# Moving small work about in a four-layer graph network: mask rows, one relu, chain distances and small loads

## The chip, the cores and the metric

One core of a Trainium2 chip runs the whole kernel. The metric is the device time of one execution in microseconds, taken as the median of several runs. The engines that matter are TensorE (PE, with its weight loads PEld), VectorE (DVE), ScalarE (ACT), GpSimd (POOL) and SyncE (SP), which issues most DMAs. Each engine works through its own instructions in the order in which the program emitted them.

## What is computed

A node has 64 features, there are 3327 nodes, and a dense 3327 x 3327 adjacency matrix with about half a per cent of non-zero entries is given in full. Four residual layers follow each other, each on a layernorm and relu of the features:

```python
h = relu(layernorm(x)); x = x + relu(ggc(relu(ggc(h, adj, ...)), adj, ...))   # L0: two gated steps
h = relu(layernorm(x)); x = x + ranked(adj) @ (h @ W) + b                      # L1
h = relu(layernorm(x)); x = x + three times: (adj*adj) @ h, then @ W.T + b     # L2
h = relu(layernorm(x)); x = x + twice: tanh(concat([adj @ h, h]) @ W)          # L3
```

`ggc` is a gated unit: m = adj @ (x W), then sigmoid gates r and z, n = tanh(i_n + r h_n), and (1 - z) n + z x. `ranked(adj)` replaces the entries of a row by powers of one half: the last non-zero of the row has the weight 1, the one before it 0.5, and so on for at most 100 of them. So all in all there are eight products with the adjacency matrix or something made from it. The kernel numbers them k = 0 to 7: 0 and 1 are L0, 2 is L1, 3 to 5 are L2, 6 and 7 are L3.

## The kernel before, in words

**Tiles.** The 3327 nodes are padded to 3328, that is 26 blocks of 128. A pair of blocks, b and b + 13, is laid side by side, so the destinations form 13 double blocks, split in four chunks (`CH`) of 3, 3, 3 and 4 double blocks: widths 384, 384, 384 and 512. Chunks 0 and 1 are group 0, chunks 2 and 3 are group 1. A `Tile` is 128 source nodes by all destinations of one group: 128 x 1536 floats (768 KB) for group 0 and 128 x 1792 (896 KB) for group 1. The matrix doesn't fit on the chip, so tiles come from memory again and again: 9 sweeps of 26 tiles, 234 loads, into 20 slots (`dead` is the list of free slots). A slot is free again when its last user has been emitted.

**Stages.** `alone(0, 0)` does product 0 for group 0. Then `joint(g, k)` uses each tile of a group for product k and, some tiles later, for product k + 1, so that one load serves both: group 1 with k = 0 and 1, group 0 with 1 and 2, group 1 with 2 and 3, and so on, till `alone(0, 7)`. The sources of the other group come first, the group's own sources last, since own features of product k + 1 are only known when product k of that group has been finished.

**The ranked product (k = 2).** A mask of a tile (`make_mask`) is 1 where the tile is not 0. It is made by VectorE in two halves (L411), the `pieces`, which wait in a queue and are emitted one by one between the units of work (`mask_pieces`). It has 127 rows of its own; row 128 (L416) gets the number of non-zeros in later blocks, from `totals`, by a DMA that GpSimd issues. TensorE multiplies the mask by a triangular matrix `tri` (L255), which counts non-zeros behind each entry. A relu with a bias then turns the count into the bits of a power of two (`e`), on ScalarE (L461) or on VectorE (L459), and TensorE multiplies it by the features in three bf16 terms (L546). `totals` comes from earlier counting of the masks by TensorE (L481).

**What sets the order.** All engines' orders are written out by `run()` (L652). It walks a list of units (product, chunk, tile): before each it emits loads as far as slots are free, prepares masks up to 44 units ahead, emits `expand` (L255 and the relus) for up to four units ahead, then pieces of masks, then the unit's own matmuls. Beside the units run tasks, written as generators: when one says `yield 2.2`, its next step is emitted as soon as units worth 2.2 us by the code's own costs (`spend`, L322) have been emitted. So a yield is a distance in emission order: it gives the other engines time to finish a step before TensorE comes to the next. A step is emitted at the end of the unit in which its distance runs out. If a result is needed before its task is through, `finish` emits the rest at once.

**The tasks that matter.** `after_0` and `after_1` run when products 0 and 1 of a chunk are complete: `gru` (L781) takes the sum out of PSUM (L741 on ScalarE, L742 on VectorE), makes the gates (L792, L797), r and n (L802, L804, L813) and the new state (L817 to L819). In cell 0 a relu of two halves follows: ScalarE writes one half (L822), VectorE the other (L823), and TensorE transposes both to node order (L707). In cell 1 `after_1` goes on with a transpose (L717, recorded on L255), the residual (L770), the layernorm (`layernorm_relu`, L751 to L765, with the power on GpSimd at L761) and a split of the features in three bf16 terms (`in_three`, L841 on ScalarE and L843 on VectorE). `more_constants` (L190) loads the weights of the cells, `bd` and `w3` (small rows of 256 B, L232 and L234) and the bias rows `brow` (L238), and folds the first weights of a cell into its gates (`fold_cell`). `bd` is first used after product 2, `w3` after product 6 and `brow[:, 0:3]` after product 2.

Of the kernel before, what the change touches and what calls it, by code (L numbers as in the profile page):

```python
# [13 lines left out]
ALU = mybir.AluOpType  # L14
# [81 lines left out]
def kernel(  # L96
# [93 lines left out]
    def more_constants():  # L190
# [38 lines left out]
        load_cell(1)  # L229
        yield 10.0  # L230
        for h in range(2):
            nc.sync.dma_start(out=bd[upper(h), :, upper(h)], in_=weights[:, WL1:WL3])  # L232
            for i in range(2):
                nc.sync.dma_start(out=w3[upper(h), :, i], in_=weights[:, WL3 + (h + i) % 2:NW:2])  # L234
        yield 10.0
        yield from fold_cell(1)
        yield 20.0
        nc.sync.dma_start(  # L238
# [166 lines left out]
    def make_mask(t, kind):  # L405

        t.mask = Mask(t.w)
        rows = P - 1 if kind == RANKED else P

        def piece(half):  # L410
            nc.vector.tensor_scalar(t.mask.view[:rows, half], t.view()[:rows, half], 0.0, None, op0=ALU.not_equal)  # L411
            if half == 0 and kind == RANKED:

                for ch in GROUPS[t.g]:
                    finish(("count", ch))
                nc.gpsimd.dma_start(out=t.mask.view[P - 1:P], in_=totals[t.g][t.q:t.q + D + 1:D, :])  # L416
            if half == 1:
                t.used()

        pieces.extend([(t, 0, piece), (t, 1, piece)])  # L420

# [7 lines left out]
    def expand(k, c, t):  # L429
# [23 lines left out]
        for s in range(2):  # L453
# [3 lines left out]
            busy = any((k - 1, ch) in sums for ch in GROUPS[t.g])  # L457
            if s and (own if t.g == 0 and (own or busy) else c == GROUPS[t.g][1] or t.g == 1 and not own):
                nc.vector.tensor_scalar(wide[:, s], ps[:, :w], BITS, 0.0, op0=ALU.add, op1=ALU.max)  # L459
            else:  # L460
                nc.scalar.activation(wide[:, s], ps[:, :w], AF.Relu, bias=bitsb)  # L461
# [319 lines left out]
    def gru(acc, c, bi, bh, cell, pace=1.0):  # L781
# [37 lines left out]
        nc.vector.tensor_tensor(d, d, r, ALU.add)  # L819
        yield 2.2 * pace  # L820
        if cell == 0:
            nc.scalar.activation(both[c][upper(1), 0], d[upper(1)], AF.Relu)  # L822
            nc.vector.tensor_scalar(both[c][upper(0), 1], d[upper(0)], 0.0, None, op0=ALU.max)  # L823
            yield 1.0 * pace
        return at, d

    parts = {}

    def in_three(h, c):

# [8 lines left out]
        for i in range(2):  # L839
            yield 0.8  # L840
            nc.scalar.copy(terms[i], h)  # L841
# [28 lines left out]
    def after_1(c, acc):  # L870
        pace = 1.0 if c in GROUPS[0] else 1.2
        at, h2T = yield from gru(acc, c, BI2, BH2, 1, pace)
# [134 lines left out]
```

## Time and profile before

| what | value |
|---|---|
| median of three runs | 721.32 us (717.43 to 722.89) |
| the profiled execution | span 714.8 us |
| adjacency tiles loaded | 130 of 768 KB, 104 of 896 KB |
| read from memory | 199.68 MB, 281 GB/s over the span |
| L546 on f32 tiles | 532.6 us busy |
| L546 on the ranked tiles | 72.6 us busy |
| L411, masks on VectorE | 114.8 us busy, 603 ns each |
| L416, rows of masks | 52 DMAs, 31.9 us on GpSimd |

The page gives each engine's busy time and, for each group of instructions, its busy time, the mean length of one and how long the engine had been idle before it, with what ended that wait. Busy times of different engines overlap and don't add up to the span; matmuls overlap each other too. A wait is worth time only where it holds up the engine that sets the end. The timeline of an engine lists its instructions with the start in us from the start of the span, the length, and in brackets the idle time before. Tile and slot names are printed without their numbers: all 20 slots are `adj`, whether they hold a tile, a mask or something of a gated unit.

### The profile page before, as it was taken

The numbers are of one execution on the slowest core, as the hardware profiler recorded it, in microseconds if no ns is written. First come the engines' busy times: TensorE is split into PE (matmuls) and PEld (weight loads), VectorE is DVE, ScalarE is ACT, GpSimd is POOL, SyncE is SP. The second block draws the span as 40 slices with busy tenths as digits, with TensorE's granted clock in tenths as the row PEclk, the third lists the DMA queues.
The fourth block names the chain that finished last, engine by engine and source line by source line (L and its number), as shares of the span: only waits on it lengthen the run. The fifth ranks groups of instructions, "written<-read, shape, count | busy, mean of one in ns | idle before, by whom it ended". The sixth has DMA issues, their size and how long they took to land.

```text
span 714.8 us, 12622 instructions
## 1 busy us (share of the span) xinstructions
PE 685.6 (96%) x5112; PEld 344.0 (48%) x5112; DVE 344.0 (48%) x696; ACT 264.1 (37%) x402; POOL 76.7 (11%) x113
## 2 busy tenths in 40 slices
PE   4999899999999898999999999999999999999997
PEld 1545444555546586545444444334444444334464
DVE  6756636634987988658524102321163566005101
ACT  0114000212037666888998223740065600000101
POOL 3500000001390602121100000000010000000000
PEclk9999999999999999999999999999999999999999
DMA  9999996299586367662999749962998399927991
GB/s 347 401 363 404 405 406 196 64 351 397 186 298 236 115 205 262 211 239 72 313 368 366 255 146 408 405 263 79 375 373 259 113 397 405 404 82 263 403 402 39
DMA packets 69109, 201.54 MB, mean 282 GB/s; under 512 B 7404, under 2 KB 8788, under 8 KB 69052
## 3 DMA queue, kind: packets, MB, share of 16 engines
q1 hardware_dynamic: 66156, 199.70, 75.4%
q8 instruction: 40, 0.66, 0.4%
q10 hardware_dynamic: 720, 0.85, 0.3%
q0 software_dynamic: 2176, 0.20, 0.2%
q14 instruction: 17, 0.14, 0.1%
HBM read 199.68 MB, written 0.85 MB: 281 GB/s over the span
## 4 chain that ended last, share of the span: by engine, by line
PE 55%; DVE 2%; DMA 2%; ACT 0%; issue 0%; POOL 0%; ACTq 0%; DVEq 0%; SPq 0%; POOLq 0%
PE sum L546 51%; PE temp L255 3%; DMA adj<-totals 1%; PE temp L707 1%; DMA adj<-in_adjT 1%; DVE adj L411 1%; DVE both L742 0%; ACT both L741 0%; DVE e L459 0%; POOL st L761 0%; PE sum L255 0%; DVE xs L940 0%; DVE y L765 0%; DVE y L758 0%; DVE t L753 0%
## 5 line engine op out<-in xcount | busy, mean ns | idle before, releaser
L546 PE MATMUL sum<-adj,y 128*64 128x384 f32 (+3 forms) x3016 | 532.6, 503 | 13.2 <-DMA adj<-in_adjT 12.2
L546 PEld LDWEIGHTS sum<-adj,y 128*64 128x64 f32 x3016 | 221.5, 137 | 267.8 <-issue 223.9
L388 ACT ACTIVATE adj<-adj 128x768 f32<-128x768 f32 (+1 forms) x173 | 141.9, 891 | 50.3 <-PE sum L546 26.9
L411 DVE TENSOR_SCALAR adj<-adj 128x768 bf16<-128x768 f32 (+3 forms) x208 | 114.8, 603 | 33.5 <-PE temp L481 29.6
L461 ACT ACTIVATE e<-temp,bitsb 128x384 int16<-128x384 f32 (+1 forms) x114 | 65.3, 606 | 23.5 <-PE temp L255 14.6
L546 PE MATMUL sum<-e,adj 128*64 128x384 bf16 (+1 forms) x624 | 72.6, 339 | 0.6 <-DVE e L459 0.6
L742 DVE COPY both<-sum 64x384 f32<-64x384 f32 (+3 forms) x17 | 9.7, 569 | 118.7 <-ACT both L741 117.5
L741 ACT COPY both<-sum 64x384 f32<-64x384 f32 (+3 forms) x17 | 8.1, 477 | 155.2 <-PE sum L546 155.1
L390 DVE TENSOR_TENSOR adj<-adj 128x768 f32<-128x768 f32 (+1 forms) x35 | 33.6, 1006 | 51.1 <-DMA adj<-in_adjT 30.9
L255 PE MATMUL temp<-adj,tri 128*64 128x384 bf16 (+1 forms) x334 | 51.9, 342 | 5.5 <-DVE e L459 2.3
L761 POOL TENSOR_TENSOR st<-st,mhalf 128x6 f32<-128x6 f32 (+1 forms) x16 | 24.0, 1500 | 295.5 <-DVE st L760 295.5
L546 PEld LDWEIGHTS <-adj 128*64 128x64 bf16 x624 | 40.4, 110 | 18.5 <-issue 6.4
L416 POOL DMA_DIRECT2D adj<-totals x52 | 31.9, 615 | 133.5 <-DVE adj L819 75.0
L459 DVE TENSOR_SCALAR e<-temp 128x384 int16<-128x384 f32 (+1 forms) x53 | 31.8, 606 | 21.2 <-ACT e L461 8.6
L255 PEld LDWEIGHTS <-tri 128*64 128x64 bf16 x416 | 28.6, 109 | 25.8 <-issue 12.8
L736 DVE STREAM_TRANSPOSE both<-y 32x96 f32<-32x96 f32 (+1 forms) x128 | 35.6, 278 | 2.9
L688 DVE COPY t<-sum 128x384 f32<-128x384 f32 x8 | 4.4, 555 | 61.3 <-PE sum L546 61.3
L481 PE MATMUL temp<-adj,behind 128*64 128x384 bf16 x208 | 28.8, 339 | 0.6 <-DVE adj L411 0.4
L686 ACT COPY t<-sum 128x384 f32<-128x384 f32 (+1 forms) x8 | 4.2, 528 | 53.7 <-PE sum L546 53.7
L481 PEld LDWEIGHTS <-behind 128*64 128x64 bf16 x208 | 13.6, 110 | 21.1 <-issue 19.5
L903 DVE TENSOR_TENSOR y<-temp,brow 128x384 f32<-128x384 f32 (+1 forms) x8 | 4.7, 591 | 29.6 <-PE temp L255 29.6
L515 ACT ACTIVATE lastw<-adj,bitsb 128x768 int16<-128x768 f32 (+1 forms) x2 | 2.0, 984 | 44.1 <-DVE adj L513 44.1
(113 smaller groups left out, 330.1 us busy)
## 6 DMA issues: line engine op xcount, KB each, us to landing
adj<-in_adjT SPq DMA_DIRECT2D x130, 768.0 KB, 7.8
adj<-in_adjT SPq DMA_DIRECT2D x104, 896.0 KB, 12.4
xs<-in_x SPq DMA_DIRECT2D x1, 640.0 KB
adj<-totals POOLq DMA_DIRECT2D x26, 3.0 KB, 4.9
adj<-totals POOLq DMA_DIRECT2D x26, 3.5 KB, 3.0
out<-xs ACTq DMA_DIRECT2D x2, 192.0 KB, 4.0
folds<-in_weights SPq DMA_DIRECT2D x4, 64.0 KB, 12.1
out<-xs ACTq DMA_DIRECT2D x1, 256.0 KB
```

The costliest lines, as they stand in the source:

```text
L255: nc.tensor.matmul(out[hs], lhsT[:, hs], rhs, start=start, stop=stop)
L388: nc.scalar.activation(sq, v, AF.Square)
L390: nc.vector.tensor_tensor(sq, v, v, ALU.mult)
L411: nc.vector.tensor_scalar(t.mask.view[:rows, half], t.view()[:rows, half], 0.0, None, op0=ALU.not_equal)
L416: nc.gpsimd.dma_start(out=t.mask.view[P - 1:P], in_=totals[t.g][t.q:t.q + D + 1:D, :])
L459: nc.vector.tensor_scalar(wide[:, s], ps[:, :w], BITS, 0.0, op0=ALU.add, op1=ALU.max)
L461: nc.scalar.activation(wide[:, s], ps[:, :w], AF.Relu, bias=bitsb)
L481: nc.tensor.matmul(counts[c][1][s * D:(s + 1) * D, :w], behind[:, NQ - 1 - t.q:NQ - 1 - t.q + D], t.mask.view[:, s, t.cols(c)], start=firs ...
L546: nc.tensor.matmul(acc[h][1][h * D:(h + 1) * D, :w], yq[h], rhs[h], start=first and n == 0, stop=last and n == len(terms) - 1)
L736: nc.vector.transpose(to[at:at + 32, :, q], h[q * 32:(q + 1) * 32, :, s, f * 32:(f + 1) * 32])
L742: nc.vector.tensor_copy(both[c][upper(1), 1], acc[1][1][upper(1), :width(c)])
L761: nc.gpsimd.tensor_tensor(st[:, 3, :n], st[:, 2, :n], mhalf[:, :n], ALU.pow)
```

## The change

Five edits are made together; none changes what is computed or how many instructions there are.

1. Rows of masks ahead: the DMA that fills row 128 of a ranked mask is issued when the mask is planned (`make_mask`), not when its first piece is emitted.
2. The relu of cell 0: VectorE's half is emitted right behind L819, with no distance between. ScalarE's half stays behind the distance, which becomes 2.4 for 2.2; the one after it no longer scales with `pace`.
3. Relus of the ranked product: in group 1, for own tiles of chunk 2, the second relu of a unit of chunk 2 goes to VectorE. For own tiles of chunk 3 it stays on ScalarE.
4. Longer distances: `after_1` runs with pace 1.25 for all chunks (before: 1.0 in group 0, 1.2 in group 1), and the distance ahead of each copy in `in_three` is 1.2 for 0.8. The aim is that VectorE's work of the two chains of group 0 doesn't crowd the relus of the ranked product.
5. Small rows later: the loads of `bd` and `w3` are moved behind the fold of cell 1 and 40 further; `brow` follows 5 later.

```diff
         yield 50.0
         load_cell(1)
-        yield 10.0
+        yield 20.0
+        yield from fold_cell(1)
+        yield 40.0
         for h in range(2):
             nc.sync.dma_start(out=bd[upper(h), :, upper(h)], in_=weights[:, WL1:WL3])
             for i in range(2):
                 nc.sync.dma_start(out=w3[upper(h), :, i], in_=weights[:, WL3 + (h + i) % 2:NW:2])
-        yield 10.0
-        yield from fold_cell(1)
-        yield 20.0
+        yield 5.0
         nc.sync.dma_start(
             out=brow[:, 0:3],
...
         def piece(half):
             nc.vector.tensor_scalar(t.mask.view[:rows, half], t.view()[:rows, half], 0.0, None, op0=ALU.not_equal)
-            if half == 0 and kind == RANKED:
-
-                for ch in GROUPS[t.g]:
-                    finish(("count", ch))
-                nc.gpsimd.dma_start(out=t.mask.view[P - 1:P], in_=totals[t.g][t.q:t.q + D + 1:D, :])
             if half == 1:
                 t.used()
 
+        if kind == RANKED:
+
+            for ch in GROUPS[t.g]:
+                finish(("count", ch))
+            nc.gpsimd.dma_start(out=t.mask.view[P - 1:P], in_=totals[t.g][t.q:t.q + D + 1:D, :])
         pieces.extend([(t, 0, piece), (t, 1, piece)])
...
-            if s and (own if t.g == 0 and (own or busy) else c == GROUPS[t.g][1] or t.g == 1 and not own):
+            alone = own and chunk_of(t.q % NB) == GROUPS[1][1]
+            if s and (own if t.g == 0 and (own or busy) else c == GROUPS[t.g][1] or t.g == 1 and not alone):
                 nc.vector.tensor_scalar(wide[:, s], ps[:, :w], BITS, 0.0, op0=ALU.add, op1=ALU.max)
...
         nc.vector.tensor_tensor(d, d, r, ALU.add)
-        yield 2.2 * pace
+        if cell == 0:
+            nc.vector.tensor_scalar(both[c][upper(0), 1], d[upper(0)], 0.0, None, op0=ALU.max)
+        yield 2.4 * pace
         if cell == 0:
             nc.scalar.activation(both[c][upper(1), 0], d[upper(1)], AF.Relu)
-            nc.vector.tensor_scalar(both[c][upper(0), 1], d[upper(0)], 0.0, None, op0=ALU.max)
-            yield 1.0 * pace
+            yield 1.0
         return at, d
...
-    def in_three(h, c):
+    def in_three(h, c, pace=1.0):
...
         for i in range(2):
-            yield 0.8
+            yield 1.2 * pace
             nc.scalar.copy(terms[i], h)
...
     def after_1(c, acc):
-        pace = 1.0 if c in GROUPS[0] else 1.2
+        pace = 1.25
         at, h2T = yield from gru(acc, c, BI2, BH2, 1, pace)
```

## The prediction

> **What bounds the kernel now.** I read the page's first part, then the list of TensorE's waits, then the timelines of the engines around each wait, and last the chain of waits.
>
> ```profile
> span 714.8 us, 12622 instructions
> PE 685.6 (96%) x5112; PEld 344.0 (48%) x5112; DVE 344.0 (48%) x696; ACT 264.1 (37%) x402; POOL 76.7 (11%) x113
> ...
> PE sum L546 <- DMA adj<-in_adjT: 12.2, 7, 8.3
> PE temp L255 <- DVE e L459: 2.3, 3, 1.6
> PE temp L255 <- DMA adj<-totals: 2.2, 2, 1.1
> PE sum L707 <- DVE both L823: 2.1, 1, 2.1
> ```
>
> TensorE is busy 96% of the span. It stands for 714.8 - 685.6 = 29.2 us in all, of which 8.3 us are the first load and about 4 us the tail after the last matmul; no edit touches either. What is left, some 17 us or 2.3%, is all that a change of order can win, since no matmul is removed. So each edit is priced by the wait of TensorE that it can end. Four places matter: the relu (77 us), the late tile (130 us), the crowded VectorE (225 to 250 us), and the two waits for rows of masks (285 and 317 us).
>
> The relu, as TensorE and VectorE saw it (start, length, instruction; in brackets the idle time before it and who ended it):
>
> ```profile
> 77.05 0.80 PE L707 MATMUL sum<-ident,both 128*64 128x64 f32 x20 [2.13 <-DVE both L823]
> ...
> 72.23 0.56 DVE L819 TENSOR_TENSOR adj<-adj 128x384 f32<-128x384 f32 x1
> 76.65 0.34 DVE L823 TENSOR_SCALAR both<-adj 64x384 f32<-64x384 f32 x1
> ```
>
> Its input was ready at 72.79, yet it ran at 76.65: VectorE first worked off the next chunk's L817 to L819 and three masks that the code had put before it.
>
> The late tile, with SyncE's issues before it, and the same wait one stage later:
>
> ```profile
> 129.82 0.87 PE L546 MATMUL sum<-adj,y 128*64 128x384 f32 x4 [1.28 <-DMA adj<-in_adjT]
> ...
> 124.08 0.62 SPq L232 DMA_DIRECT2D bd<-in_weights  x1
> 124.75 1.26 SPq L234 DMA_DIRECT2D w<-in_weights  x2
> ...
> 212.40 1.51 PE L546 MATMUL sum<-adj,y 128*64 128x384 f32 x8 [0.75 <-DMA adj<-in_adjT]
> ```
>
> The last adjacency tile of group 1 is issued at about 123.45 us (its issue ends at 124.02), right ahead of six loads of small rows, and lands about 6.3 us later.
>
> The stretch with both of group 0's chains: three of TensorE's waits, then busy time by window.
>
> ```profile
> 234.51 0.35 PE L255 MATMUL temp<-adj,tri 128*64 128x384 bf16 x2 [0.44 <-DVE e L459]
> 235.50 0.35 PE L255 MATMUL temp<-adj,tri 128*64 128x384 bf16 x2 [0.65 <-DVE xs L770]
> 241.36 0.35 PE L255 MATMUL temp<-adj,tri 128*64 128x384 bf16 x2 [1.64 <-DVE e L459]
> 225.00:250.00 25.00, 21.23 (x265) 15.68 (x263) 24.04 (x52) 18.12 (x37) 11.13 (x16) 1.00 0.41 147
> ```
>
> The columns of the last line are the stretch, its length, then PE, PEld, DVE, ACT and POOL. VectorE works 24.04 of 25 us and TensorE only 21.23, so here VectorE is the bound. TensorE's waits between 223 and 250 us sum to 0.22 + 0.44 + 0.65 + 0.58 + 1.64 + 0.20 = 3.7 us.
>
> **What the Trainium skill says.** "PSUM — Partial Sum Buffer", section "Engine vs sequencer instructions": the queues of ScalarE, VectorE and GpSimdE are strictly first in, first out. The relu above agrees: ready at 72.79, run at 76.65. "DMA: Bandwidth & Descriptors", section "Specifications": transfers under 512 B don't reach line rate. The rows of `bd` and `w3` are 256 B each; the tile that shared the queues with them took about 6.3 us where the first load after the quiet stretch, of the same 896 KB, took 5.1 (237.89 to 242.96). The same page, section "Anatomy of one DMA — SWDGE (gpsimd) path", gives a DMA issued from GpSimd about 2.0 us of fixed cost; here the 52 rows of masks took 1.6 us at least, 4.0 in the median, 6.0 at most. So a row must be issued some 4 us ahead to be free.
>
> **The change, part by part.**
>
> *Half of the relu at once.* L823 moves in front of the yield, behind L819. It then ends at 72.79 + 0.34 = 73.13 us. TensorE reaches L707 at 74.5 (its first four matmuls, on ScalarE's half, start at 74.51), so the wait of 2.13 goes. The next chunk's chain slides by 0.34 us, and its own relu half is done at about 76.4, while TensorE, 2.1 us earlier, wants it at 78.70 - 2.13 = 76.6: at most 0.1 us. The yield of 2.4 for 2.2 doesn't move the step, as both run out within the same unit of the schedule. Does the gain last? Adjacency tiles land every 2.2 us, and TensorE spends 3.2 + 0.2 us on one when both layers use it (L546 x16 in 3.18, then L481), so tiles pile up and no load limits it till the late tile, whose issue waits on masks and counts that move with TensorE. **Gain 2.0 us**, between 1.0 and 2.1.
>
> *Small rows later.* The six loads leave the late tile alone. At 5.0 us from issue it lands at 128.5, when TensorE has ended the work before it (129.82 - 1.28 = 128.54): gain 1.28, at least 0.6. Where do they go? Walking the schedule with the code's own costs, load and fold of cell 1 stay where they were, and the six loads come 40 later: between the 75th and the 76th tile load, that of `brow` between the 77th and the 78th. The 78th is the one that lands at 212.40 and is waited for already. SyncE issues the 75th at 198.46 and the 76th at 201.61, so six issues of 0.65 us each (124.08 to 128.0) push the 76th to about 203.0, and the 78th from 205.62 to 206.2. Their packets took 1.3 us of all 16 DMA engines' time, `brow`'s 0.3, in a stretch whose DMA share was 0.9 to 1.0. So the 78th lands 0.3 to 2.5 us later; I take 1.1, since some of its wait is for slots. **Net gain 0.2 us**, between -1.9 and +1.0.
>
> *Longer distances.* No work is added, only order. In steps of the code, group 0's chain of after_1 takes 6.6 x 1 + 1.2 x 4 + 3.2 + 1.5 = 16.1 before, and 6.8 x 1.25 + 1.5 x 4 + 4.0 + 1.5 = 20.0 after. That is 3.9 more between the end of layer 1's sum and the node features that layer 2 needs. Group 1's grows by 1.6 and has over 10 to spare. What it can win is the 3.7 us above, what limits it is VectorE's total: 24.04 us of work in 25. The longer chain moves about 1.6 us of it (three L843 of 0.54) behind the first unit that needs it, and moves some 2 us of early chain work into the full stretch. What it can lose is the far end: chunk 0's last L843 ends at 244.47, and the first unit that reads it starts at 250.23. Of these 5.8 us the change takes 3.9 and a faster TensorE up to 3.7 more, so a stall of up to 2 us may replace the waits. **Gain 1.2 us**, between -2.0 and +3.5.
>
> *Rows of masks ahead.* Only the place of 52 issues in GpSimd's queue changes; in group 0 by one unit of 0.65, in group 1's last tiles by up to 3.5. Behind an issue that waits for its buffer can stand the power of the layernorm (L761, 1.35 us) and the rows of `lasty`. The two waits for rows come from here:
>
> ```profile
> 281.48 1.32 POOL L761 TENSOR_TENSOR st<-st,mhalf 128x6 f32<-128x6 f32 x1 [7.03 <-DVE st L760]
> 282.76 1.20 POOL L416 DMA_DIRECT2D adj<-totals  x2
> ...
> 312.39 2.39 POOL L416 DMA_DIRECT2D adj<-totals  x4 [8.42 <-ACT e L461]
> ```
>
> The first stood behind L761, which the code emits before that mask is made in either version. The second waited for its buffer, and its mask is made and its first piece emitted in the same turn of run(). Neither is issued earlier. The masks' own VectorE work (L411) never waited for a row, as VectorE's list of waits has none for `totals`, so the turned order adds no wait there. **Gain 0.1 us**, between -0.8 and +2.2.
>
> *Relu of chunk 2's own tiles.* For six units of chunk 2 the second relu goes from ScalarE to VectorE, 0.6 us on either (L461 606 ns, L459 606 ns). TensorE didn't wait for ScalarE there. VectorE has gaps of 1.6 to 3.4 us up to 318 us, few after, and ten masks of 329 us lie on the chain of waits: **loss 0.1 us**, between -0.8 and +0.3 as a gain.
>
> Sum: 2.0 + 0.2 + 1.2 + 0.1 - 0.1 = 3.4 us, or 0.5%. From the median of 721.32 this gives **717.9 us**.
>
> **The rivals.** *Everything ends*: 2.1 for the relu, 1.28 for the tile with nothing paid at 212 us, 3.5 of the chains' waits and 2.2 of the rows'. That is 9.1 us, so 712.2. For it speaks that each named wait has an edit aimed at it; against it, the two rows whose cause isn't touched, and VectorE's 24.04 of 25 us. *New waits take the place of the old*: the relu and the tile win 3.3, but the 78th tile lands 2.5 us later, the first own units stall 3.0 us for features that come late, and the relus on VectorE cost 0.8. That is 3.0 lost, net of the gains: 721.32 - 3.3 + 6.3 = 724.3, slower. For it speaks that both hits fall on waits and margins seen above; against it, that both need the worst bound at once. *Only the relu counts* (2 us, the rest even): 719.3, inside the forecast.
>
> **From the cases to the numbers.** The forecast, with the relu alone as its weak form, gets 0.66, everything ends 0.19, new waits 0.15. The predicted time is the forecast's. The range reaches from 712.5 (nearly the full gain) to 723.0 (past no change): the bounds of the single terms give this, and the three runs before lie 5.5 us apart. Faster by over 1% means under 714.1: most of the second case, 0.14. Slower by over 1% means over 728.5, beyond even the worst sum: 0.04. Within 1%: 0.82.
>
> **What would show it.** Right: no wait of L707 for L823 near 77 us; L546 not waiting near 127 us; a wait for a tile near 209 us of 1 to 3 us; both waits for rows still about 1.1 us each; waits of L255 for L459 and L770 between 220 and 247 us down from 3.7 to about 2.5. Wrong: a wait of the first own unit of layer 2 over 2 us, the rows' waits gone, or a wait of L411 for a row. The forecast fails if tiles turn out to limit TensorE between 80 and 200 us, since then the first 3 us are given back.

## The result, and the profile after

The changed kernel took **724.71 us** (median; 721.83 to 727.44), the kernel before 720.82 us beside it on the same chip. The ratio is **1.0049, 95% interval 1.0034 to 1.0064**: the change made the kernel slower by some 3.5 us. The forecast was 717.9 us, with a range up to 723.0.

Single executions of one kernel lie 6 to 8 us apart here, and the two profiled ones lie at opposite ends: 716.73 us for the kernel before, 727.13 for the changed one. So the traces show which waits there are; what an edit is worth is read from the ratios, which rest on all the executions. The page of the changed kernel, first part:

```profile
span 725.3 us, 12627 instructions
PE 690.7 (95%) x5112; PEld 360.6 (50%) x5112; DVE 346.7 (48%) x702; ACT 261.7 (36%) x396; POOL 76.7 (11%) x113
```

TensorE stands for 725.3 - 690.7 = 34.6 us, where it was 29.2, and it is busy 5.1 us longer with the same 5112 instructions. Part of this second sum is a lower clock, which comes below. The top of the list of TensorE's waits (engine, line, what was waited for: us in all, times, longest):

```profile
PE sum L547 <- DMA adj<-in_adjT: 14.3, 8, 8.3
PE temp L255 <- DMA adj<-totals: 4.9, 2, 3.1
PE temp L255 <- DVE e L460: 2.4, 4, 0.8
```

Lines have moved by one to three: L546 is L547, L459 is L460, L481 is L482, L802 and L804 are L803 and L805, L817 to L819 are L818 to L820, L770 is L771, L823 is L822. The wait of L707 for the relu is gone; waits for tiles and rows have grown, those for `L805` and `L771` have grown or are new. These waits on TensorE's timeline:

```profile
78.23 0.32 PE L482 MATMUL temp<-adj,behind 128*64 128x384 bf16 x1 [0.51 <-DVE adj L411]
128.93 0.87 PE L547 MATMUL sum<-adj,y 128*64 128x384 f32 x4 [0.17 <-DMA adj<-in_adjT]
214.72 2.00 PE L547 MATMUL sum<-adj,y 128*64 128x384 f32 x8 [3.58 <-DMA adj<-in_adjT]
232.54 0.77 PE L255 MATMUL temp<-adj,tri 128*64 128x384 bf16 x4 [2.07 <-DVE adj L805]
245.16 0.35 PE L255 MATMUL temp<-adj,tri 128*64 128x384 bf16 x2 [1.53 <-DVE xs L771]
293.25 0.52 PE L255 MATMUL temp<-adj,tri 128*64 128x384 bf16 x4 [3.05 <-DMA adj<-totals]
326.90 0.52 PE L255 MATMUL temp<-adj,tri 128*64 128x384 bf16 x4 [1.81 <-DMA adj<-totals]
```

**Relu and late tile** did as forecast in the main: 2.13 us became 0.72, now for masks (0.51 here and 0.21 just behind; the forecast had at most 0.1), and 1.28 became 0.17. **The 78th tile** is waited for 3.58 us (and 0.15 just before) instead of 0.75. SyncE's own timeline shows what stands ahead of it:

```profile
197.58 0.54 SPq L353 DMA_DIRECT2D adj<-in_adjT  x1
198.17 0.62 SPq L234 DMA_DIRECT2D bd<-in_weights  x1
198.84 1.26 SPq L236 DMA_DIRECT2D w<-in_weights  x2
200.15 0.61 SPq L234 DMA_DIRECT2D bd<-in_weights  x1
200.80 1.28 SPq L236 DMA_DIRECT2D w<-in_weights  x2
202.19 2.42 SPq L353 DMA_DIRECT2D adj<-in_adjT  x2
204.66 0.60 SPq L238 DMA_DIRECT2D brow<-in_bias_rows  x1
205.35 1.20 SPq L353 DMA_DIRECT2D adj<-in_adjT  x2
```

The 75th is the load issued at 197.58, the 78th the one at 205.35; before, they were issued at 198.46 and 205.62. So the loads run a little earlier here, and counted from the 75th the 78th comes after 7.77 us for 7.16: the 0.6 us that the forecast had for the delay of the issue. The larger part is on its way: in the stretch 195 to 210 us the transfers moved 252, 276 and 316 GB/s before, 235, 239 and 280 after. The middle one of the three stretches, before and after (the last two numbers are the share of the DMA engines and GB/s):

```profile
200.00:205.00 5.00, 5.00 (x38) 2.34 (x34) 5.00 (x11) 2.55 (x6) 4.94 (x8) 1.00 0.84 276
200.00:205.00 5.00, 5.00 (x40) 2.42 (x38) 5.00 (x11) 2.64 (x5) 3.97 (x6) 1.00 0.85 239
```

By 5 us each that is 0.45 MB less, over half a tile, and 0.26 MB of what was moved after are the small rows themselves. So the tiles queued ahead of the 78th, and it with them, come later.

**The chains.** TensorE now waits 2.07 us for `L805`, a reader of a PSUM bank that it wants to write. VectorE's timeline ahead of that wait:

```profile
228.48 0.56 DVE L460 TENSOR_SCALAR e<-temp 128x384 int16<-128x384 f32 x1 [2.72 <-PE temp L255]
229.07 1.12 DVE L818 TENSOR_TENSOR adj<-both,adj 64x384 f32<-64x384 f32 x2
230.22 0.56 DVE L819 TENSOR_TENSOR adj<-adj 128x384 f32<-128x384 f32 x1
230.81 0.56 DVE L820 TENSOR_TENSOR adj<-adj 128x384 f32<-128x384 f32 x1
231.29 0.61 DVE L803 SCALAR_TENSOR_TENSOR adj<-temp,bcol,adj 128x384 f32<-128x384 f32 x1
```

L818 to L820 are the last step of chunk 0's gated unit. Before, VectorE did them at 222.19 to 224.5, ahead of the relu for which it then waited 0.71 us:

```profile
222.19 1.12 DVE L817 TENSOR_TENSOR adj<-both,adj 64x384 f32<-64x384 f32 x2
...
225.21 0.56 DVE L459 TENSOR_SCALAR e<-temp 128x384 int16<-128x384 f32 x1 [0.71 <-PE temp L255]
```

With the longer distances they stand behind that relu: VectorE idles 2.72 us, then works 2.2 us on chunk 0 while chunk 1's L803 and L805, and the bank with them, are held up. Its full stretch doesn't go, it only comes later. In the changed kernel VectorE works 24.54 us of the 25 from 241 us on; in the version without edit 5 (below), where no half clock falls into the stretch, the busy times (VectorE's is the third) are:

```profile
231.00:256.00 25.00, 19.81 (x258) 15.55 (x255) 24.44 (x51) 16.39 (x33) 9.93 (x13) 1.00 0.30 98
```

### The profile page after: what moved, and what is told of

Same layout as the page of the kernel before. It is cut to its first block, busy times and chain, and to the rows that moved or that the text cites. A ratio compares the mean times of both kernels' runs of the same rounds, so it can differ in the third digit from the quotient of the medians.

```text
span 725.3 us, 12627 instructions
## 1 busy us (share of the span) xinstructions
PE 690.7 (95%) x5112; PEld 360.6 (50%) x5112; DVE 346.7 (48%) x702; ACT 261.7 (36%) x396; POOL 76.7 (11%) x113
## 4 chain that ended last, share of the span: by engine, by line
PE 51%; ACT 4%; DMA 2%; DVE 1%; issue 1%; ACTq 0%; DVEq 0%
PE sum L547 47%; ACT adj L388 4%; PE temp L255 3%; DMA adj<-totals 1%; DVE adj L411 1%; PE temp L708 1%; DMA out<-xs 1%; DVE both L743 0%; ACT both L742 0%; DVE xs L942 0%; ACT t L687 0%; PE sum L255 0%; ACT t L939 0%; ACT e L462 0%; ACTq L944 0%
## 5 line engine op out<-in xcount | busy, mean ns | idle before, releaser
L547 PE MATMUL sum<-adj,y 128*64 128x384 f32 (+3 forms) x3016 | 537.1, 505 | 15.2 <-DMA adj<-in_adjT 14.3
L547 PEld LDWEIGHTS sum<-adj,y 128*64 128x64 f32 x3016 | 232.8, 138 | 261.9 <-issue 213.9
L547 PE MATMUL sum<-e,adj 128*64 128x384 bf16 (+1 forms) x624 | 73.6, 342 | 0.6 <-DVE e L460 0.6
L462 ACT ACTIVATE e<-temp,bitsb 128x384 int16<-128x384 f32 (+1 forms) x106 | 61.2, 601 | 34.0 <-PE temp L255 17.8
L547 PEld LDWEIGHTS <-adj 128*64 128x64 bf16 x624 | 41.6, 111 | 18.9 <-issue 6.8
L460 DVE TENSOR_SCALAR e<-temp 128x384 int16<-128x384 f32 (+1 forms) x61 | 36.3, 602 | 23.4 <-PE temp L255 14.2
L482 PE MATMUL temp<-adj,behind 128*64 128x384 bf16 x208 | 31.2, 340 | 1.3 <-DVE adj L411 1.2
L482 PEld LDWEIGHTS <-behind 128*64 128x64 bf16 x208 | 17.7, 111 | 18.4 <-issue 16.7
```

Of the source, the lines that this page charges most:

```text
L482: nc.tensor.matmul(counts[c][1][s * D:(s + 1) * D, :w], behind[:, NQ - 1 - t.q:NQ - 1 - t.q + D], t.mask.view[:, s, t.cols(c)], start=firs ...
L547: nc.tensor.matmul(acc[h][1][h * D:(h + 1) * D, :w], yq[h], rhs[h], start=first and n == 0, stop=last and n == len(terms) - 1)
```

## Single edits

Each edit alone, in the kernel before. Edit 5, small rows later:

```diff
-        yield 10.0
+        yield 20.0
+        yield from fold_cell(1)
+        yield 40.0
         for h in range(2):
             nc.sync.dma_start(out=bd[upper(h), :, upper(h)], in_=weights[:, WL1:WL3])
...
-        yield 10.0
-        yield from fold_cell(1)
-        yield 20.0
+        yield 5.0
```

> The kernel before with the small rows later alone. Theory 'small rows' (the loads of bd, w3 and brow now share the queues with the 78th tile): L546's wait for the late tile near 130 us goes (1.28 to at most 0.3), the wait for the 78th tile near 212 us grows from 0.75 to 3 us or more, and a pause of that length is followed by a stretch of half clock on TensorE of about 3.4 us (some 1.7 us lost): 2 to 4 us slower than before, ratio 1.003 to 1.005. Rivals 'chains' and 'rows': this edit is about even, ratio 0.999 to 1.001.

Edit 2, the relu:

```diff
-        yield 2.2 * pace
         if cell == 0:
-            nc.scalar.activation(both[c][upper(1), 0], d[upper(1)], AF.Relu)
             nc.vector.tensor_scalar(both[c][upper(0), 1], d[upper(0)], 0.0, None, op0=ALU.max)
-            yield 1.0 * pace
+        yield (2.4 if cell == 0 else 2.2) * pace
+        if cell == 0:
+            nc.scalar.activation(both[c][upper(1), 0], d[upper(1)], AF.Relu)
+            yield 1.0
```

> The kernel before with the relu's half at once alone (the distances behind it as in the changed kernel, cell 0 only). All theories: the wait of L707 near 77 us goes; the masks that follow are 0.3 to 0.7 us late for L481, so the gain is 1.2 to 2.0 us: ratio 0.997 to 0.9985.

Edit 4, longer distances:

```diff
-        yield 2.2 * pace
+        yield (2.2 if cell == 0 else 2.4) * pace
...
-            yield 0.8
+            yield 1.2
             nc.scalar.copy(terms[i], h)
...
-        pace = 1.0 if c in GROUPS[0] else 1.2
+        pace = 1.25
```

> The kernel before with the longer distances alone (pace 1.25, 2.4 in cell 1, 1.2 in in_three). Theory 'chains' (a chain that is drawn out holds its PSUM banks for more units, so L255 waits for the bank till L804 or L770 has read it, and then the clock halves): TensorE's waits between the end of product 1 in group 0 and the first own unit rise from 3.7 to about 6 us, with one stretch of half clock: 2 to 4 us slower, ratio 1.003 to 1.006. Theory 'small rows': even, 0.999 to 1.001.

Edit 1, rows of masks ahead:

```diff
-            if half == 0 and kind == RANKED:
-                for ch in GROUPS[t.g]:
-                    finish(("count", ch))
-                nc.gpsimd.dma_start(out=t.mask.view[P - 1:P], in_=totals[t.g][t.q:t.q + D + 1:D, :])
...
+        if kind == RANKED:
+            for ch in GROUPS[t.g]:
+                finish(("count", ch))
+            nc.gpsimd.dma_start(out=t.mask.view[P - 1:P], in_=totals[t.g][t.q:t.q + D + 1:D, :])
         pieces.extend([(t, 0, piece), (t, 1, piece)])
```

> The kernel before with the rows of masks issued ahead alone. Theory 'rows' (the issue order on GpSimd makes rows land later): the two waits for rows, 2.2 us before, become about 4.9 us as in the changed kernel, with half clock behind the longer one: 2.7 to 4.4 us slower, ratio 1.004 to 1.006. Theory 'small rows' or 'chains': waits for rows stay near 1.1 us each, ratio 0.999 to 1.001, and the long waits for rows in the changed kernel come from where tile loads fall in time.

Edit 3, the relus of chunk 2:

```diff
-            if s and (own if t.g == 0 and (own or busy) else c == GROUPS[t.g][1] or t.g == 1 and not own):
+            alone = own and chunk_of(t.q % NB) == GROUPS[1][1]
+            if s and (own if t.g == 0 and (own or busy) else c == GROUPS[t.g][1] or t.g == 1 and not alone):
```

> The kernel before with the fifth part alone: in group 1, the second relu of chunk 2's own tiles on VectorE. Theory 'clock' (the changed kernel is slower mainly because more of TensorE's pauses are long enough to be followed by 3.4 us of half clock; the small rows, the chains and the rows of masks cause them): this part makes no pause, ratio 0.999 to 1.001. Rival 'VectorE is full at 320 us': masks come late, L255 waits for L411 or L459 for 1 to 3 us between 317 and 335 us, ratio 1.002 to 1.004.

| edit alone | ratio to before (95%) | in us | waits in its trace |
|---|---|---|---|
| small rows | 1.0024 (1.0001 to 1.0047) | +1.7 | late tile 0.71; 78th tile 0.99 and 2.39 |
| relu | 0.9962 (0.9941 to 0.9983) | -2.7 | L481 for masks 0.73, in place of L707's 2.13 |
| distances | 1.0014 (0.9993 to 1.0035) | +1.0 | 219 to 262 us: 6.0 for 3.7 |
| rows ahead | 1.0017 (0.9999 to 1.0036) | +1.2 | 219 to 262 us: 4.4; rows 2.93 and 1.77 |
| chunk 2's relus | 0.9997 (0.9978 to 1.0016) | -0.2 | its time alone is used |

The relu alone makes the kernel faster, small rows alone slower, though its interval only just lies above 1; each of the other three can't be told from no change by itself. The five sum to 1.0 us, give or take some 3, so they neither contradict the 3.5 us nor account for them.

## One edit undone, or placed otherwise, in the changed kernel

Four versions of the changed kernel: without edit 5, without edit 4, without edit 1, and with edit 5 only half done, the rows of `bd` and `w3` right behind the fold:

```diff
         yield 20.0
         yield from fold_cell(1)
-        yield 40.0
         for h in range(2):
             nc.sync.dma_start(out=bd[upper(h), :, upper(h)], in_=weights[:, WL1:WL3])
...
-        yield 5.0
+        yield 20.0
         nc.sync.dma_start(
             out=brow[:, 0:3],
```

The other three put the lines of edits 5, 4 and 1 back as they were.

> The changed kernel with the loads of bd, w3 and brow put back to their old places. Theory 'small rows': the wait for the 78th tile falls from 3.7 to about 1.3 us and with it one stretch of half clock; the late tile waits 1 us again: 1 to 3 us faster than the changed kernel, so ratio to the kernel before 1.001 to 1.003. Rival (the sum of the other parts is what costs): ratio 1.004 or more.

> The changed kernel without the longer distances: the pace of after_1 and the distances of in_three are as before. If the chains cost 1.5 to 2 us (waits 5.9 for 3.7 us, and a half-clock stretch of 1.7 us behind the one of 2.07 us), the wait for L805 near 232 us goes and the ratio to the kernel before is 1.001 to 1.003. If they are worth nothing by themselves and the small rows cost everything, it stays at 1.004 to 1.006. If the longer distances gain what was forecast (1.2 us), it rises to 1.006 to 1.007.

> The changed kernel with one edit undone: the row of a mask is issued with the mask's first piece, as before. If the rows ahead cost what they seemed to alone (1.0017, within its interval nothing), the ratio is 1.002 to 1.005; the waits for rows near 293 and 327 us stay, at 1 to 3.5 us each. If the rows ahead are what makes these two waits long, both fall to 1.1 us and the ratio to 1.000 to 1.002.

> The changed kernel with one thing different: the six loads of bd and w3 go right behind the fold of cell 1 (not 40 later), and brow keeps its old distance of 20. If the small rows, by way of the 78th tile, cost what the changed kernel loses, the wait near 215 us falls from 3.58 to about 1.2 us, no half-clock stretch follows it, and the time is 3 to 4 us under the changed kernel: 720.5 to 721.5, a ratio to the kernel before of 0.998 to 1.001. If the chains (waits of L255 for L805 and L771, 5.9 us) cost it, the wait near 215 us may go but the ratio stays at 1.003 to 1.005.

And, from the kernel before, the relu together with the small rows right behind the fold (the two edits already shown):

> The kernel before with the relu's half at once, and with the loads of bd and w3 behind the fold of cell 1 with no further distance: between the 54th and the 55th tile load, brow where it was. Theory 'small rows' (what costs is that they share the queues with a tile that is just in time; tiles 53 to 60 land over 8 us ahead of their use): the late tile's wait near 128 us is at most 0.4 us and the 78th's stays near 1 us; 2 us for the relu and 1 us for the tile, ratio 0.994 to 0.996. Rival (the wait for the 78th tile doesn't come from the small rows): it is again over 2.5 us, ratio 0.998 or more.

| version | ratio to before (95%) |
|---|---|
| changed kernel | 1.0049 (1.0034 to 1.0064) |
| without small rows later | 1.0010 (0.9990 to 1.0031) |
| without longer distances | 1.0019 (1.0000 to 1.0038) |
| without rows ahead | 1.0028 (1.0006 to 1.0049) |
| small rows right behind the fold | 0.9996 (0.9976 to 1.0016) |
| before, with relu and small rows right behind the fold | 0.9967 (0.9945 to 0.9990) |

In company, small rows cost 0.0049 - 0.0010, or 2.8 us, the distances 2.2 and the rows 1.5, each give or take 2, so that the rows may cost nothing. (A second measurement of the changed kernel, below, gave 1.0068; against it each is 1.4 us more.) Moved 40 earlier, the small rows give back the whole loss: late tile 0.42, 78th tile 1.34 us. That confirms the place of the loads as a cause. In this trace, though, the wait at the first row's place is also shorter, 1.20 us for 3.05; since it was 1.17 in a second trace of the changed kernel, this may be chance, and what share of the return it has isn't shown. The loads aren't the only cause: without the distances the wait of 2.07 us went, and the ratio fell as expected for that. Without rows ahead the two waits for rows stayed, at 3.41 and 2.00 us, so this edit isn't what makes them long. And beside the relu, small rows right behind the fold add nothing that can be told: 0.9967 for 0.9962 with the relu alone, whose trace has only 0.31 us left for the late tile.

Which loads delay the 78th tile, `bd` and `w3` or `brow`? In the next one, from the kernel before, the first are loaded after `brow`, which keeps its distance from the fold, so no small row stands right ahead of the 78th tile:

```diff
-        for h in range(2):
-            nc.sync.dma_start(out=bd[upper(h), :, upper(h)], in_=weights[:, WL1:WL3])
-            for i in range(2):
-                nc.sync.dma_start(out=w3[upper(h), :, i], in_=weights[:, WL3 + (h + i) % 2:NW:2])
...
         yield from fold_cell(1)
         yield 20.0
         nc.sync.dma_start(
             out=brow[:, 0:3],
...
+        yield 20.0
+        for h in range(2):
+            nc.sync.dma_start(out=bd[upper(h), :, upper(h)], in_=weights[:, WL1:WL3])
+            for i in range(2):
+                nc.sync.dma_start(out=w3[upper(h), :, i], in_=weights[:, WL3 + (h + i) % 2:NW:2])
```

> The kernel before with one thing different: bd and w3 are loaded after brow, 20 later, and brow keeps its old distance from the fold. If the six loads of bd and w3 (3.9 us of issue ahead of the 76th tile) make the 78th tile late, its wait is about 2.4 to 3 us as with the whole edit, and the ratio is 1.001 to 1.004. If brow, whose 128 small packets lie right ahead of the 78th tile in the changed kernel, makes it late, the wait is 0.75 to 1.5 us as before, the late tile's wait of 1.28 us falls, and the ratio is 0.998 to 1.000.

The ratio was 1.0011 (0.9992 to 1.0030), and on TensorE's timeline:

```profile
214.20 0.89 PE L546 MATMUL sum<-adj,y 128*64 128x384 f32 x4 [2.24 <-DMA adj<-in_adjT]
216.16 2.83 PE L546 MATMUL sum<-adj,y 128*64 128x384 f32 x8 [1.07 <-DMA adj<-in_adjT]
```

3.3 us in all, as with the whole edit (3.4 alone), so the six loads of `bd` and `w3` do it, ahead of the 76th tile; `brow` isn't needed for it. Nor is a late issue: here the 78th is issued 7.17 us behind the 75th, as before. The ratio alone would not have shown it, as its interval includes 1. Over the traces of all kernels run, the waits for tiles at this place come to 3.0 us or more, 3.3 in the mean, in the six with late small rows and no other work put in (changed kernel twice, edit 5 alone, this one, no distances, no rows), and to 0.75 to 2.06 us, 1.4 in the mean, in the ten that load them earlier. So the edit adds 1.9 us there; the 0.75 that the forecast started from was the lowest of all.

## What a long pause does to the clock

Behind three of the pauses above the trace shows a lower clock. Busy time in stretches of the changed kernel (stretch, length, then PE, PEld, DVE, ACT, POOL, granted clock of TensorE, share of the DMA engines, GB/s):

```profile
215.00:220.00 5.00, 5.00 (x24) 2.08 (x22) 2.06 (x4) 1.91 (x4) 0.21 (x1) 0.66 0.78 269
295.00:300.00 5.00, 5.00 (x33) 2.18 (x32) 2.32 (x4) 2.75 (x5) 0.54 (x1) 0.75 0.08 17
```

The records have it as half clock for 3.41 us at a time, from 215.60, 232.67 and 294.11: within 0.9 us behind the waits of 3.58, 2.07 and 3.05 us. Before, there was none but in the tail. To see the cost by itself, VectorE was made to repeat an idempotent maximum in two hops of the kernel before (12 instructions more in all), so that TensorE has to wait where it is otherwise the bound:

```diff
             m = evacuate(acc, c)
+            for _ in range({3: 4, 4: 8}[k] if c == 0 else 0):
+                nc.vector.tensor_tensor(m, m, m, ALU.max)
             yield 0.8
```

> The kernel before with two pauses of TensorE put in where nothing else waits: four extra maxima of VectorE (0.56 us each, they change nothing) on the sum of chunk 0 after product 3, eight after product 4. TensorE waits for them at about 414 us for 1.2 to 1.8 us and at about 438 us for 3.3 to 4.0 us. Theory 'clock': the granted clock stays full after the short pause and is half for 3.4 us after the long one, in which the matmuls of L546 take about twice as long, so the span grows by the pauses and by 1.7 us more. Rival (the half clock comes from something else, such as the amount of work): full clock after both.

TensorE's timeline, then a stretch behind the second pause:

```profile
421.04 0.88 PE L255 MATMUL temp<-bd,t 128*64 128x128 f32 x12 [1.74 <-DVE t L899]
448.61 1.55 PE L255 MATMUL temp<-bd,t 128*64 128x128 f32 x12 [4.11 <-DVE t L899]
```

```profile
448.00:452.00 4.00, 3.39 (x22) 2.22 (x24) 1.11 (x2) 0.00 (x0) 0.00 (x0) 0.58 1.03 406
```

Behind 1.74 us the clock stayed full, behind 4.11 it was halved. The transpose L707 that began at 637.50 us before began at 650.54 here, 13.04 later; ahead of the pauses the lag was 5.42 (L546 at 348.00 and 353.42). Of the 7.62 us between, 5.85 are the pauses themselves and **1.77 the half clock**, near to half of 3.41. It was not caught up. The execution took 729.76 us.

When does it come? The half-clock stretches of one trace all begin on a grid of 3.41 us, which lies otherwise in each execution. In 19 traces (changed kernel twice, all other kernels that were profiled here but one), over 3,767 periods of this grid between 20 and 700 us, I summed TensorE's idle time in each. All 30 periods with 1.98 us or more were followed by one at half clock. Of those with 1.91 us or less only two were, and both were themselves at half clock. So in these traces the limit lies between 1.91 and 1.98 us of idle time within one period, and where the grid lies decides whether a wait of 2 to 3 us falls into one period or is split. L707's wait of 2.13 us was split in the profile of before (1.91 in one period), with no effect, and brought half clock in the kernels with only the rows ahead, and with `brow` kept.

The Trainium skill, "TensorE: Matmul & The Clock Gate", section "What's actually happening", describes this: a clock gate with two states, half and full, set by a free-running activity window of 3413 ns. The traces agree on both numbers. It names an idle window of about 3.4 us as what throttles; here 1.98 us of idle time in it were enough.

## Is the half clock what the change lost?

By the mean granted clock of the timed executions, the changed kernel loses (1 - 0.9924) x 720 = 5.5 us to it, the kernel before 2.3. The difference is nearly the whole loss, so I took it for the cause and tried to remove it with no wait removed: useless matmuls (`ident` by `ident`, into a bank that is overwritten next) right ahead of the matmuls that wait.

```diff
+    def fill(n):
+        i = idle_temps[0]
+        for _ in range(n):
+            mm(banks[i][:, :P], ident, ident)
...
+        if len(rows_of) > 32 and t is rows_of[32] and c == GROUPS[t.g][0]:
+            fill(5)
...
+        if len(loads) > 77 and t is loads[77] and k != COUNT and (k, c) == (1, GROUPS[t.g][0]):
+            fill(7)
```

> The changed kernel with work added and none taken away: right ahead of the matmuls that wait for the 78th tile TensorE does 14 useless matmuls (64x128 f32, ident by ident, into a bank that the next user overwrites), right ahead of those that wait for the first late row 10 of them: by the length of L547 about 1.7 and 1.2 us. They leave the ends of both waits where they were and cut the idle time in them from 3.58 to about 1.9 us and from 3.05 to about 1.9 us. If the half-clock stretches behind these pauses cost time, one or both go, and the kernel with more work is 2 to 3.5 us faster than the changed one: a ratio to the kernel before of 1.000 to 1.002. If the waits alone cost the time and the clock only comes along, it stays at 1.004 to 1.006; if the added work counts, 1.006 to 1.009.

On TensorE's timeline the first filling took 1.70 us, the wait behind it was 2.10, and the half clock at this place was gone:

```profile
210.55 1.70 PE L255 MATMUL temp<-ident 128*64 128x128 f32 x28
214.35 1.51 PE L559 MATMUL sum<-adj,y 128*64 128x384 f32 x8 [2.10 <-DMA adj<-in_adjT]
```

Yet the ratio was 1.0055 (1.0032 to 1.0078), though the mean clock gave back 3.2 us. The next versions were the changed kernel again, three fillings (`fill(6)`, and `fill(4)` ahead of each of the two late rows), and the same three in places where TensorE doesn't wait (`loads[59]`, `rows_of[35]`, `rows_of[38]`):

> The changed kernel, for the same chip and hour as the next two: a ratio to the kernel before of 1.004 to 1.006, half-clock stretches of 3.41 us behind pauses of over 2 us, and waits of 2.5 to 3.7 us for the 78th tile, 2 for L805, 1 to 3.5 for each of the two rows.

> The changed kernel with 12, 8 and 8 useless matmuls right ahead of those that wait for the 78th tile, the first and the second late row: 1.46, 1.0 and 1.0 us of work, by the 1.70 us that 14 of them took. If half clock costs time and the waits are longer than the added work, nearly all of it goes (mean clock 0.998 for 0.992) and the time is 3 to 4 us under that of the changed kernel. If the added work costs what the clock gains, or the time saved is waited for at the next load, the time is within 1 us of it. If the added work is simply added, it is 3 us over it.

> The changed kernel with the same 12, 8 and 8 useless matmuls in other places: ahead of a tile of the third sweep and of the 36th and the 39th mask, where TensorE didn't wait in any profile. The half-clock stretches stay. If TensorE is the bound there, the added 3.5 us are added: a ratio of 1.009 to 1.011 to the kernel before. If the next wait gives them back (a tile or a row that comes at its own time), less: 1.005 to 1.007.

| kernel | ratio to before (95%) | median us | lost to half clock by the mean clock, us |
|---|---|---|---|
| changed kernel again | 1.0068 (1.0043 to 1.0093) | 724.61 | 6.6 |
| three fillings in the pauses | 1.0052 (1.0029 to 1.0076) | 724.09 | 2.0 |
| the same elsewhere | 1.0072 (1.0048 to 1.0095) | 725.85 | 3.4 |

The theory fell in this form: 4.6 us of half clock taken away brought 0.5 us in the median, 1.2 give or take 2.5 by the ratios. And the same fillings elsewhere, which were expected to leave the half clock as it was, went along with 3.2 us less of it and no gain in time. One reason is shown by the traces. From the wait for L805 to that of 1.53 us for L771 it is 12.62 us in the changed kernel (232.54 to 245.16), with a half-clock stretch in between, and 12.53 with the first fillings, with none (230.48 to 243.01). There the chain on VectorE sets the time; at full clock TensorE waits 1.23 us more for L771 (L783 in this version) in between:

```profile
236.83 0.35 PE L255 MATMUL temp<-adj,tri 128*64 128x384 bf16 x2 [1.23 <-DVE xs L783]
```

So this half-clock stretch cost 0.1 us and not 1.7. Behind the 78th tile it did cost: from there to the wait for L805 it is 17.82 us in the changed kernel and 16.13 with the fillings. How much of the 3.5 us is half clock in the median stays open, since the fillings may themselves cost time in executions whose waits are short, and no run separates that. (Elsewhere they cost 1.2 us by the medians, 0.3 by the ratios, where 3.5 were added; the wait for the 78th tile was 1.57 us there.)

The single executions on record with their clock give a bound of sorts. At a mean clock of 0.996 or 0.997 three of the changed kernel took 723.0 us in the mean, 85 of the kernel before 721.2; at 0.993 to 0.995 it was 724.8 (8 of them) and 723.9 (65). So at the same clock the changed kernel still takes 0.9 to 1.9 us more, and at most the rest of the 3.5 us goes along with its lower clock.

## The place of the power on GpSimd

Both waits for rows stayed, as forecast, but they are not 1.1 us each. In the kernel with the two pauses, which is the kernel before up to 400 us, they were 2.22 and 2.14; over all traces in which TensorE waited for it the first was 1.0 to 3.5. The forecast's reason was that this row stands behind the power L761 in GpSimd's queue. A longer distance in one layernorm, chunk 1 behind product 2 (5.25 for 1.5; the second expectation below names product 1 and a distance of 3.5, but its edit is this one), moves the second power behind the row:

```diff
-        yield from layernorm_relu(yk, c, pace=1.0)
+        yield from layernorm_relu(yk, c, pace=3.5 if c == GROUPS[0][1] else 1.0)
```

> The kernel before with one thing different: the distance in the layernorm of chunk 1 behind product 2 is 5.25 for 1.5, so that the row of a mask stands ahead of the second power in GpSimd's queue. If the row's place behind both powers makes the first wait for a row, that wait (1.1 us in one trace of this program, 2.2 in another) falls under 0.5 us and the ratio is 0.996 to 0.998. If the gain of the combined version came from the other two edits, it is 0.999 to 1.001 here.

> The kernel before with the relu at once, bd and w3 right behind the fold of cell 1, and a longer distance in the layernorm of chunk 1 behind product 1 (3.5 where there is 1.5), so that one row of a mask is issued ahead of the second power on GpSimd and not behind both. If the place of the row in GpSimd's queue sets the wait of TensorE near 285 us, that wait falls from 1.1 us (up to 3 in other runs) to under 0.5 us and the ratio is 0.992 to 0.995. If the row's own flight behind the tile load in front of it sets the wait, the wait stays at 0.7 to 3 us, and the ratio is that of the relu and the early small loads together, 0.995 to 0.998.

GpSimd's timeline with this edit alone, then TensorE's:

```profile
273.87 1.35 POOL L761 TENSOR_TENSOR st<-st,mhalf 128x6 f32<-128x6 f32 x1 [22.48 <-DVE st L760]
275.19 0.64 POOL L416 DMA_DIRECT2D adj<-totals  x1
285.08 1.58 POOL L761 TENSOR_TENSOR st<-st,mhalf 128x6 f32<-128x6 f32 x1 [9.25 <-DVE st L760]
```

```profile
285.50 0.35 PE L255 MATMUL temp<-adj,tri 128*64 128x384 bf16 x2 [1.38 <-DVE adj L411]
317.26 0.52 PE L255 MATMUL temp<-adj,tri 128*64 128x384 bf16 x4 [1.26 <-DMA adj<-totals]
```

The row is issued at 275.19 in place of 282.76, and TensorE waits for the mask itself, 1.38 us. **This edit alone gives 0.9950 (0.9934 to 0.9966), 3.6 us.** The wait wasn't expected to be that long (under 0.5 us), nor the gain that large. In this trace the two waits at the rows' places are 1.38 + 1.26 = 2.6 us with full clock behind both, in the two traces of the kernel before 2.2 us with full clock and 4.4 with half clock behind both; the mean clock of all its executions is 0.9987, for 0.9962 of the kernel before beside it. So the gain is partly shorter waits and partly clock; how much is which isn't shown.

Together with the relu and the small rows right behind the fold it gives 716.39 us, **0.9924 (0.9894 to 0.9954)**: faster than both kernels. Of its waits between 60 and 345 us none is above 1.8 us, its mean clock is 0.9997, and its seven executions lie within 2.2 us of each other (715.68 to 717.91), the 60 of before within 10 (718.16 to 728.44).

## Why the prediction was wrong

- **Relu: right.** Forecast gain 2.0, measured 2.7 (1.2 to 4.2). The wait went; 0.73 us of waiting for masks came, where the forecast had at most 0.1 for the next chunk. So the waits there explain 1.4 us, and the fit of the size may be in part luck.
- **Small rows: wrong size, wrong sign.** Forecast net gain 0.2, measured loss 1.7 alone. The gain term was smaller by the waits, 0.7 for 1.28 (late tile: 0.31 in the mean with late small rows, for 1.0 with neither this edit nor the relu's). The loss term was larger: 1.1 taken, 1.9 measured by the waits. The small rows' packet time (1.3 and 0.3) and the delay of the issue (0.6) sum to 2.2, close to it; the step that failed is the discount to 1.1, "since some of its wait is for slots". With `brow` kept the wait came without the delay, so the bytes on the way weigh more than the issue.
- **Longer distances: the step that failed outright.** Forecast gain 1.2, measured loss 1.0 alone (-0.5 to 2.5, so not clear of zero) and 2.2 in company. "It can win the 3.7 us above, what limits it is VectorE's total": that total hardly changed. In 25 us VectorE worked 24.04 us before, 24.44 in the changed kernel without edit 5 and 24.54 in the changed kernel, some 10 us later. The crowd stayed and the order got worse: L818 to L820 fell behind a relu that wasn't ready, and banks stayed taken. The loss I did look for, the first own unit, didn't come. Waits between 219 and 262 us were 3.7 us in all eight kernels with neither this edit nor rows ahead, 6.0 and 6.4 with this one and not the rows, 4.4 with the rows and not this one, 7.3 with both where no half clock fell into them.
- **Rows of masks: gain 0.1 forecast, 1.2 lost** (-0.1 to 2.6), 1.5 in company, neither clear of zero. The reason for the first of the two waits was right, as moving the power ended the wait for the row; that for the second wasn't tested. The 0.6 us that the turned order adds at 240 us was not seen. **Chunk 2's relus:** 0.1 lost forecast, 0.2 gained, both nothing.
- **Missing:** a term for the half clock. Each wait was priced at its length. Where TensorE is the bound, one of 2 us or more in one period costs up to 1.8 us more. What this adds to the 3.5 us stays open, as shown above.

The rival "new waits take the place of the old", with 724.3, had the number and one of its three causes: the 78th tile. The stall of the own units and the cost of the relus didn't come; the waits for banks did. From the waits, the sum is -1.4 (relu) - 0.7 (late tile) + 1.9 (78th tile) + 2.3 to 3.6 (chains, without and with rows ahead) = 2.1 to 3.4 us, by 3.5 measured. That leaves out the half clock and the two waits for rows, so the fit is no proof. By the ratios, the relu's 2.7 gained and the 2.8, 2.2 and 1.5 that small rows, distances and rows cost in company make 3.8, each give or take 2.

## What to carry to other kernels

Where one engine is nearly full, longer emission distances don't thin its work out; they only put each step behind other instructions: look at what it will stand behind, whether that can block, and which bank or buffer is held meanwhile. Small loads moved out of one wait need a place where the DMA engines aren't nearly full (0.74 to 0.97 busy here), not only one where nobody waits at the moment; and a wait read from one trace may be the smallest of its kind. Where a wait stands behind an instruction of another task in an engine's queue, move that instruction: here one distance gained 3.6 us, where the five edits lost 3.5.

## What was not expected of the hardware

TensorE's clock is halved for 3.41 us behind each period of a 3.41 us grid in which it stands for 1.98 us or more (30 of 30, none at 1.91 us or less at full clock). The grid lies differently in each execution. That may be one source of the up to 10 us between executions of one kernel: in the kernel before, the 50 at a mean clock of 0.999 or 1.000 took 718.9 us in the mean, the 17 at 0.993 took 725.6; but longer waits come with the lower clock, and no run here parts the two. And a half-clock stretch can be free, 0.1 us, where another engine sets the time. In all 19 traces the first late row landed 0.16 to 0.19 us behind a tile load. Why that load takes 5.0 us in some executions and 7.5 in others stays open.
